# Two of four scans of a Mamba layer take their start value as a 513th column

## The chip, the cores and the metric

The kernel runs on one core of a Trainium2 chip. The metric is the device time of one execution in microseconds, in the runs before a median of 7167.19 us (three runs, 7165.84 to 7173.1). Engines: TensorE (PE; PEld is its weight load), VectorE (DVE), ScalarE (ACT), GpSimd (POOL) and SyncE (SP, which here issues DMAs). Each works off its own queue of instructions in order; semaphores make them wait for each other.

## The reference

Input: x, 4 images of 128 channels x 128 x 128. Layer 0 is a Mamba block over L = 16384 tokens per image, layer 1 a spectral layer (group norm, FFT, filter, inverse FFT). The change touches only the scan of layer 0:

```
A = -exp(A_log)                                  # 256 channels x 16 states
def step(h, (d_t, B_t, C_t, u_t)):               # over the 16384 tokens, in order
    dA = exp(d_t[:, :, None] * A)
    h  = h * dA + d_t[:, :, None] * B_t[:, None, :] * u_t[:, :, None]
    y  = einsum('bds,bs->bd', h, C_t)
```

Before it: an MLP, a projection, a convolution over four tokens with SiLU (u), and the projections to d (softplus), B and C. After it: y + u*D, times silu(z), an output projection, group norm, SiLU and a residual.

## The kernel before, in words

**Chunks, units, places, slots.** A chunk k is 512 tokens (T) of one image; 128 chunks run one after another (4 images x 32). The 256 channels x 16 states of a chunk are 4096 recurrences, which lie in 32 tiles of 128 partitions: 4 states (SQ) x 32 channels (DG). A unit (j, r) with j in 0, 1 and r in 0..3 holds four of these tiles, its places p = 0..3 (state group p, channel group place(r, p)). Two slots make a unit: the even slot n holds places 0 and 1, the odd slot places 2 and 3. So a chunk has 8 units and 16 slots (NP).

**One place.** ScalarE makes dA as exp(scale * delta) (exps, line 393): place 0 into SBUF (two buffers), places 1 to 3 into one PSUM bank each (one buffer). dB*u comes for places 1 to 3 from GpSimd as a product into the tile hb (dbu, line 363: 1536 columns per unit in one or two instructions), and for place 0 from TensorE as four transposes of the tile bt into the PSUM bank b0 (dbu_turn, line 383). VectorE then runs the recurrence with one tensor_tensor_scan over 512 columns (line 412). It starts from the last column of the same place in the chunk before (the tile st, one value per partition), or from the constant 0.0 in the first chunk of an image. Places 2 and 3 (by_vector) are scanned in place, in PSUM, multiplied by C on VectorE (line 414) into hb, and ScalarE copies their last column to st (line 415). Places 0 and 1 are scanned into the SBUF tile h, multiplied by C on GpSimd, both in one instruction of 1024 columns (line 419), and their last columns are copied on ScalarE a slot later (the copy of h; line 554 is the place that issues it). Place 1 of unit (1, 2) goes to VectorE in odd chunks that norm no image; place 2 of that unit goes to GpSimd in the chunks that do. TensorE sums the products over the states (sums, line 433) into y.

**What sets the order.** The order of work is written out by hand: a table todo[slot, phase] of small functions, issued slot by slot and phase by phase (lines 549 to 554), and kept as issued. Each engine works in that order. In a slot the phases are turn, sums, pe, exps, late, act, pool, dbu, early, gate, scans, dve, end:
- exps: in an even slot the exponentials of places 2 and 3 of the same unit, in an odd slot that of place 1 of the next unit.
- early (odd slots): the exponential of place 0 of the unit after the next.
- late: the copy of h's last columns.
- scans: both scans of the slot, place 0 before 1 and 2 before 3, then the products and, on ScalarE, the copies of VectorE's last columns.
- act and pool: the steps that prepare the next chunk (the table at lines 322 to 331): in slot 2 the SiLU of z and of u (lines 242, 239), in slot 6 the softplus (line 275), each with its table load; in slots 8 to 14 the bt activations (line 304), and so on. ScalarE's exponentials need a table of their own, so each of these two steps has a load ahead and one behind.
- dve: the gates (line 443, slots 2 and 10) and, in 16 chunks of each image but the first, the adds and statistics that norm the image before (lines 637, 641; slot 3).

E2 and E3 (exponentials of places 2 and 3) of a unit write the banks that the products of the unit before read; E1 writes the bank that S1 (scan of place 1) read.

A chunk that norms is one with norming(k); there are 48, and 80 plain ones. Layer 1 (block1) follows from about 6410 us on and has the time to the end.

Of the kernel before, what the change touches and what calls it, by code (L numbers as in the profile page):

```python
# [33 lines left out]
P = 128  # L34
# [5 lines left out]
EARLY = 2  # L40
KEEP = 4
LAG = 7
EPS = 1e-5


# [109 lines left out]
def block0(tc, s):  # L155
# [4 lines left out]
    with ExitStack() as ctx:  # L160
# [17 lines left out]
        def turn_bank(n):  # L178
            return pst.tile([P, T], F32, tag="pt", name=f"pt_{n}")

        st = {}
        stats, outs = s.stats, s.outs

# [163 lines left out]
        def by_vector(k, j, r, p):  # L347

            if norming(k):
                return p > 1 and (j, r, p) != (1, 2, 2)  # L350
            return p > 1 or (k % 2 == 1 and (j, r, p) == (1, 2, 1))

        def dbu(u):

            k, r = divmod(u, NH * NG)
            j, r = divmod(r, NG)
            d = st[k]
            hb = d["hb", j, r] = hpool.tile([P, ND, T], F32, tag="hb", name=f"hb_{k}_{j}_{r}")
            p = 1
            while p < NG:  # L360
                m = place(r, p)
                n = min(NG - p, ND - m)
                nc.gpsimd.tensor_tensor(  # L363
                    hb[:, p : p + n, :], d["du", j][:, m : m + n, :], d["B"][:, p - 1 : p - 1 + n, :], ALU.mult
                )
                p += n

        def pair(n):

# [5 lines left out]
        def dbu_turn(n):  # L375

            k, j, r, p = pair(n)
            d = st[k]
            if p == 0:
                b = d["b0"] = psd.tile([P, T], F32, tag="b0", name=f"b0_{k}_{j}_{r}")  # L380
                for t in range(NT):
                    src = d["bt"][:, t, j * ND + place(r, 0), :, :].rearrange("p s d -> p (s d)")
                    nc.tensor.transpose(b[:, t * P : (t + 1) * P], src, s.ident)  # L383

        def exps(n, qs):

            k, j, r, p = pair(n)
            d = st[k]
            for q in qs:
                m = place(r, p + q)  # L390
                c = (j * NG + p + q) * ND + m
                da = (psd if p + q else p2).tile([P, T], F32, tag=f"da{p + q}", name=f"da{p + q}_{k}_{j}_{r}")
                nc.scalar.activation(da, d["delta", j][:, m, :], AF.Exp, scale=s.amat[:, c : c + 1])  # L393
                d["da", j, r, p + q] = da

        def scans(n):


            k, j, r, p = pair(n)
            d = st[k]  # L400
            hb = d["hb", j, r]
            das = [d.pop(("da", j, r, p + q)) for q in range(2)]
            dve = [q for q in range(2) if by_vector(k, j, r, p + q)]
            pool = [q for q in range(2) if q not in dve]
            last = d["last", j, r, p] = tiny.tile([P, 2], F32, tag=f"st{j}_{r}_{p}", name=f"st_{k}_{j}_{r}_{p}")
            if pool:
                h = p2.tile([P, 2, T], F32, tag="h", name=f"h_{k}_{j}_{r}_{p}", bufs=3)
            for q in range(2):
                b = hb[:, p + q, :] if p + q else d.pop("b0")
                init = 0.0 if k % NCH == 0 else st[k - 1]["last", j, r, p][:, q : q + 1]  # L410
                o = das[q] if q in dve else h[:, q, :]
                nc.vector.tensor_tensor_scan(o, das[q], b, init, ALU.mult, ALU.add)  # L412
            for q in dve:
                nc.vector.tensor_tensor(hb[:, p + q, :], das[q], d["C"][:, p + q, :], ALU.mult)  # L414
                nc.scalar.copy(last[:, q : q + 1], das[q][:, T - 1 : T])  # L415
            if pool:
                q = slice(pool[0], pool[-1] + 1)
                ps = slice(p + pool[0], p + pool[-1] + 1)
                nc.gpsimd.tensor_tensor(hb[:, ps, :], h[:, q, :], d["C"][:, ps, :], ALU.mult)  # L419
                todo[n + 1, "late"].append(partial(nc.scalar.copy, last[:, q], h[:, q, T - 1]))  # L420

        def sums(u):

# [7 lines left out]
            for p in range(ND):  # L431
                m = place(r, p)
                nc.tensor.matmul(  # L433
                    y[m * DG : (m + 1) * DG, :], s.sel, d["hb", j, r][:, p, :], start=False, stop=r == NG - 1
                )

        def post(k):
# [101 lines left out]
        for n in range(n_chunks * NP):  # L539
            if n % 2 == 0:  # L540
                todo[n - 3, "early"].append(partial(exps, n, (0,)))
            todo[n - 1, "exps"].append(partial(exps, n, (1,) if n % 2 == 0 else (0, 1)))
            todo[n - 1, "turn"].append(partial(dbu_turn, n))
            todo[n, "scans"].append(partial(scans, n))
            if n % 2 == 0:
                todo[n - 2, "dbu"].append(partial(dbu, n // 2))
            else:
                todo[n + 2, "sums"].append(partial(sums, n // 2))
        slots = [n for n, _ in todo]
        with tc.manual_schedule():  # L550
            for n in range(min(slots), max(slots) + 1):
                for phase in ("turn", "sums", "pe", "exps", "late", "act", "pool", "dbu", "early", "gate", "scans", "dve", "end"):
                    for f in todo[n, phase]:
                        f()

# [500 lines left out]
```

## Time and profile before

| | us |
|---|---|
| median of the runs | 7167.19 |
| the profiled execution | 7175.45 |
| its span in the profile | 7173.6 |
| busy: DVE / POOL / ACT / PE | 6892.9 / 6892.5 / 6143.9 / 5904.2 |
| scans of VectorE, 4096, mean of one | 1.21 to 1.27 |
| products of VectorE (line 414), 2040, mean | 0.674 |
| products of GpSimd (line 419), 984 of 1024 columns and 88 of 512, mean | 2.363 and 1.276 |
| exponentials (line 393), 4096, mean | 0.700 |
| table loads, each | 1.283 |

Durations of one engine overlap by some 0.06 to 0.1 us, so its load is counted in steps from start to start. A line of the timeline gives the start, the length and the operation; x2 merges two of the same kind; the bracket tells how long the engine was idle before and what it waited for. In the chain of waits a share of an engine is time in which that engine had the work that ended last.

### The profile page before, as it was taken

The page shows a single profiled execution, that of the slowest core. Times are in us where ns is not written, and L with a number is a line of the kernel's source. Part 1 is how long each engine was busy: PE and PEld are TensorE (multiplying, and loading weights), DVE is VectorE, ACT ScalarE, POOL GpSimd, SP SyncE. Part 2 cuts the span into 40 slices and gives each one's busy share as a digit, 9 for nine tenths or more (in the row PEclk, how much of TensorE's full clock was granted, in tenths as well). Part 3 has the DMA queues.
Part 4 walks back from the last instruction along what each step waited for, and adds up shares of the span by engine and source line. Part 5 has one row for each costly group of instructions (what it writes and reads, how often), then busy time and mean ns, then how long its engine had stood idle before and what let it go on. Part 6 is the DMA issues. An engine that isn't in the chain of part 4 may idle for free.

```text
span 7173.6 us, 91384 instructions
## 1 busy us (share of the span) xinstructions
PE 5904.2 (82%) x26708; PEld 2626.8 (37%) x26708; DVE 6892.9 (96%) x7966; ACT 6143.9 (86%) x13658; POOL 6892.5 (96%) x3188
## 2 busy tenths in 40 slices
PE   6888888788787788888888788888887888867998
PEld 2333333233222233333333333333333333326888
DVE  6999999999999999999999999999999999989777
ACT  6888888888888888888888888898888888878876
POOL 6999999999999999999999999999999999988887
PEclk8888888888888889998989899999898899979999
DMA  5666666666777777777777777777777777769866
GB/s 139 160 160 152 163 159 151 165 159 165 191 176 192 179 171 176 172 184 175 189 196 186 188 176 175 178 177 184 189 191 194 177 179 177 172 164 306 236 185 162
DMA packets 905480, 1286.20 MB, mean 179 GB/s; under 512 B 81672, under 2 KB 356752, under 8 KB 904976
## 3 DMA queue, kind: packets, MB, share of 16 engines
q1 hardware_dynamic: 904832, 1280.09, 71.9%
q8 instruction: 210, 3.44, 0.2%
q14 instruction: 294, 2.41, 0.1%
q10 hardware_dynamic: 144, 0.26, 0.0%
HBM read 1023.45 MB, written 256.58 MB: 178 GB/s over the span
## 4 chain that ended last, share of the span: by engine, by line
DVE 41%; ACT 29%; issue 11%; PE 10%; DMA 5%; POOL 3%; SPq 1%; DVEq 0%; ACTq 0%; POOLq 0%
DVE da L412 20%; DVE h L412 12%; ACT da L393 12%; DVE hb L414 5%; ACT L393 3%; DMA rdelta<-dd 2%; ACT L275 2%; ACT delta L275 2%; ACT bt L304 2%; POOL hb L363 2%; DVE zs L443 1%; PE y L433 1%; POOL hb L419 1%; ACT L242 1%; DMA xt<-x 1%
## 5 line engine op out<-in xcount | busy, mean ns | idle before, releaser
L363 POOL TENSOR_TENSOR hb<-rdu,rB 128x1536 f32<-128x1536 f32 (+2 forms) x1536 | 3605.7, 2364 | 22.4 <-DMA rdelta<-dd 21.3
L393 ACT ACTIVATE da<-rdelta,amat 128x512 f32<-128x512 f32 x4096 | 2794.1, 700 | 138.3 <-DVE h L412 133.9
L419 POOL TENSOR_TENSOR hb<-h,rC 128x1024 f32<-128x1024 f32 (+1 forms) x1072 | 2435.0, 2274 | 88.8 <-DVE h L412 73.4
L412 DVE TENSOR_TENSOR_SCAN da<-da,st,hb 128x512 f32<-128x512 f32 x1976 | 2419.8, 1267 | 21.5 <-ACT da L393 14.3
L433 PE MATMUL y<-hb,sel 128*32 128x512 f32 x8192 | 1313.4, 717 | 2.9 <-POOL hb L419 2.7
L414 DVE TENSOR_TENSOR hb<-da,rC 128x512 f32<-128x512 f32 x2040 | 1296.1, 674 | 3.0
L412 DVE TENSOR_TENSOR_SCAN h<-da,st,b 128x512 f32<-128x512 f32 x992 | 1258.3, 1268 | 1.7 <-PE b L383 1.6
L412 DVE TENSOR_TENSOR_SCAN h<-da,st,hb 128x512 f32<-128x512 f32 x1000 | 1251.6, 1255 | 1.8 <-ACT da L393 1.8
L383 PE MATMUL b<-ident,bt 128*128 128x128 f32 x4096 | 748.4, 305 | 516.1 <-DVE h L412 390.6
L234 PE MATMUL pp_cv<-xm,wck 128*128 128x512 f32 x2048 | 1014.3, 640 | 1.6 <-ACT xm L217 0.8
L304 ACT ACTIVATE bt<-pt_dut,xdt 128x256 f32<-128x256 f32 x2048 | 839.4, 474 | 184.5 <-PE pt_dut L293 184.3
L383 PEld LDWEIGHTS b<-ident,bt 128*128 128x128 f32 x4096 | 531.3, 154 | 1017.1 <-DVE h L412 692.8
L415 ACT COPY st<-da 128x1 f32<-128x1 f32 x2040 | 273.1, 160 | 474.2 <-DVE hb L414 471.1
L234 PEld LDWEIGHTS pp_cv<-xm,wck 128*128 128x128 f32 x2048 | 395.9, 204 | 651.0 <-issue 422.1
L828 POOL TENSOR_TENSOR wb<-wb,term 128x1040 f32<-128x1040 f32 x192 | 461.0, 2401 | 70.8 <-ACT term L822 62.9
L293 PE MATMUL pt_dut<-ident,du 128*128 128x128 f32 x1024 | 232.4, 338 | 285.1 <-ACT xdt L286 174.9
L429 PE MATMUL y<-u,diag 128*128 128x512 f32 x512 | 303.0, 675 | 188.7 <-DVE zs L443 187.3
L293 PEld LDWEIGHTS pt_dut<-ident,du 128*128 128x128 f32 x1024 | 132.2, 162 | 604.8 <-POOL du L312 475.9
L393 ACT ACT_TABLE_LOAD x262 | 336.1, 1283 | 12.1 <-DMA rdelta<-dd 7.4
L312 POOL TENSOR_TENSOR du<-delta,u 128x512 f32<-128x512 f32 x256 | 318.8, 1267 | 25.8 <-ACT delta L275 25.8
L223 PE MATMUL pp_z<-xm,win 128*128 128x512 f32 x512 | 274.5, 634 | 51.8 <-ACT fq L497 46.2
L267 PE MATMUL pp_dt<-xd,wdt 8*128 8x512 f32 x512 | 284.8, 642 | 33.0 <-ACT pp_o L457 23.5
(160 smaller groups left out, 8139.8 us busy)
## 6 DMA issues: line engine op xcount, KB each, us to landing
rdelta<-dd SPq DMA_DIRECT2D x1024, 256.0 KB, 4.7
rdu<-dd SPq DMA_DIRECT2D x1024, 256.0 KB, 7.5
rC<-bc SPq DMA_DIRECT2D x512, 256.0 KB, 7.3
rB<-bc SPq DMA_DIRECT2D x512, 192.0 KB, 4.7
dd<-delta SPq DMA_DIRECT2D x256, 256.0 KB, 7.2
dd<-du SPq DMA_DIRECT2D x256, 256.0 KB, 5.7
ft<-in_filt_w SPq DMA_DIRECT2D x104, 520.0 KB, 7.0
ob<-o SPq DMA_DIRECT2D x128, 256.0 KB, 2.1
```

The costliest lines, as they stand in the source:

```text
L234: nc.tensor.matmul(ps["cv", j], w, d["xm"][:, t : t + T], start=t == 0, stop=t == KC - 1)
L293: nc.tensor.transpose(ps["dut"][:, 2 * t + j, :], d["du"][:, j, at : at + P], s.ident)
L304: nc.scalar.activation(d["bt"][:, 2 * h + t, :, q, :], src, AF.Copy, scale=d["xdt"][:, 2 * h + t, R + q : R + q + 1])
L312: nc.gpsimd.tensor_tensor(du, d["delta"][:, j, :], d["u"][:, j, :], ALU.mult)
L363: nc.gpsimd.tensor_tensor(hb[:, p : p + n, :], d["du", j][:, m : m + n, :], d["B"][:, p - 1 : p - 1 + n, :], ALU.mult)
L383: nc.tensor.transpose(b[:, t * P : (t + 1) * P], src, s.ident)
L393: nc.scalar.activation(da, d["delta", j][:, m, :], AF.Exp, scale=s.amat[:, c : c + 1])
L412: nc.vector.tensor_tensor_scan(o, das[q], b, init, ALU.mult, ALU.add)
L414: nc.vector.tensor_tensor(hb[:, p + q, :], das[q], d["C"][:, p + q, :], ALU.mult)
L419: nc.gpsimd.tensor_tensor(hb[:, ps, :], h[:, q, :], d["C"][:, ps, :], ALU.mult)
L433: nc.tensor.matmul(y[m * DG : (m + 1) * DG, :], s.sel, d["hb", j, r][:, p, :], start=False, stop=r == NG - 1)
L828: nc.gpsimd.tensor_tensor(wb, wb, u[n].terms[f], ALU.add)
```

## The change

- Places 1 and 2 of a unit are "carried": their scan runs over 513 columns from the constant 0.0. Column 0 of the second operand holds the start value, so the first step gives 0 * a + start. hb gets 513 columns per place, and a new step carry writes column 0 of places 1 and 2: on ScalarE a copy from the chunk before, in an image's first chunk a memset on GpSimd. The columns of dA must be 513 too: b0, dA of place 1 and dA of place 2 become three banks of one PSUM tile, band, and a carried scan reads from the last column of the bank before its own. The scan of place 2, in place, overwrites that column of place 1's bank. Where place 1 goes to VectorE, places 1 and 2 are not carried.
- The waits on band are set by hand (on_band): an instruction waits for the last one of each other engine on the same bank, and for none on other banks.
- The scans of an even slot run in the order 1, 0.
- Place 1 of unit (1, 2) goes to VectorE in all chunks that norm no image.
- The exponential of place 1 of the next unit is issued at the end of the odd slot's scans, behind late, early and carry; those three and scans now come before act, pool and dbu, and the products (with the copies of last columns) in a phase of their own after dbu.
- On TensorE the transposes for place 0 come after sums, but in units with r = 2 (of 0..3) before, as they were.

```diff
--- before.py
+++ after.py
@@ -40,6 +40,9 @@
 EARLY = 2
 KEEP = 4
 LAG = 7
+PHASES = (
+    "first turn", "sums", "turn", "pe", "exps", "late", "early", "carry", "scans", "act", "pool", "dbu", "products", "dve", "end"
+)
 EPS = 1e-5
 
 
@@ -178,6 +181,28 @@
         def turn_bank(n):
             return pst.tile([P, T], F32, tag="pt", name=f"pt_{n}")
 
+        band = psd.tile([P, 3 * T], F32, tag="band", name="band")
+        users = []
+
+        def on_band(engine, banks, made):
+
+            i = made.ins
+            seen = set()
+            for e, b, j in reversed(users):
+                if e == engine:
+                    continue
+                if not b & banks:
+                    tc.declare_no_dep(i, j, reason="another bank")
+                    continue
+                for bank in b & banks:
+                    if (e, bank) not in seen:
+                        seen.add((e, bank))
+                        tc.add_manual_dep(
+                            i, j.name, mybir.DependencyInfo(mybir.DependencyClass.Sync, mybir.DependencyReason.DATA),
+                            reason="same bank",
+                        )
+            users.append((engine, banks, i))
+            del users[:-40]
         st = {}
         stats, outs = s.stats, s.outs
 
@@ -348,22 +373,37 @@
 
             if norming(k):
                 return p > 1 and (j, r, p) != (1, 2, 2)
-            return p > 1 or (k % 2 == 1 and (j, r, p) == (1, 2, 1))
+            return p > 1 or (j, r, p) == (1, 2, 1)
 
         def dbu(u):
 
             k, r = divmod(u, NH * NG)
             j, r = divmod(r, NG)
             d = st[k]
-            hb = d["hb", j, r] = hpool.tile([P, ND, T], F32, tag="hb", name=f"hb_{k}_{j}_{r}")
+            hb = d["hb", j, r] = hpool.tile([P, ND, 1 + T], F32, tag="hb", name=f"hb_{k}_{j}_{r}")
             p = 1
             while p < NG:
                 m = place(r, p)
                 n = min(NG - p, ND - m)
                 nc.gpsimd.tensor_tensor(
-                    hb[:, p : p + n, :], d["du", j][:, m : m + n, :], d["B"][:, p - 1 : p - 1 + n, :], ALU.mult
+                    hb[:, p : p + n, 1:], d["du", j][:, m : m + n, :], d["B"][:, p - 1 : p - 1 + n, :], ALU.mult
                 )
                 p += n
+
+        def carried(k, j, r):
+
+            return () if by_vector(k, j, r, 1) else (1, 2)
+
+        def carry(u):
+
+            k, r = divmod(u, NH * NG)
+            j, r = divmod(r, NG)
+            if carried(k, j, r):
+                o = st[k]["hb", j, r][:, 1:3, 0]
+                if k % NCH == 0:
+                    nc.gpsimd.memset(o, 0.0)
+                else:
+                    nc.scalar.copy(o, st[k - 1]["last", j, r][:, 1:3])
 
         def pair(n):
 
@@ -377,10 +417,10 @@
             k, j, r, p = pair(n)
             d = st[k]
             if p == 0:
-                b = d["b0"] = psd.tile([P, T], F32, tag="b0", name=f"b0_{k}_{j}_{r}")
+                b = band[:, 0:T]
                 for t in range(NT):
                     src = d["bt"][:, t, j * ND + place(r, 0), :, :].rearrange("p s d -> p (s d)")
-                    nc.tensor.transpose(b[:, t * P : (t + 1) * P], src, s.ident)
+                    on_band("PE", {0}, nc.tensor.transpose(b[:, t * P : (t + 1) * P], src, s.ident))
 
         def exps(n, qs):
 
@@ -389,8 +429,13 @@
             for q in qs:
                 m = place(r, p + q)
                 c = (j * NG + p + q) * ND + m
-                da = (psd if p + q else p2).tile([P, T], F32, tag=f"da{p + q}", name=f"da{p + q}_{k}_{j}_{r}")
-                nc.scalar.activation(da, d["delta", j][:, m, :], AF.Exp, scale=s.amat[:, c : c + 1])
+                if p + q in (1, 2):
+                    da = band[:, (p + q) * T : (p + q + 1) * T]
+                else:
+                    da = (psd if p else p2).tile([P, T], F32, tag=f"da{p + q}", name=f"da{p + q}_{k}_{j}_{r}")
+                made = nc.scalar.activation(da, d["delta", j][:, m, :], AF.Exp, scale=s.amat[:, c : c + 1])
+                if p + q in (1, 2):
+                    on_band("ACT", {p + q}, made)
                 d["da", j, r, p + q] = da
 
         def scans(n):
@@ -402,22 +447,46 @@
             das = [d.pop(("da", j, r, p + q)) for q in range(2)]
             dve = [q for q in range(2) if by_vector(k, j, r, p + q)]
             pool = [q for q in range(2) if q not in dve]
-            last = d["last", j, r, p] = tiny.tile([P, 2], F32, tag=f"st{j}_{r}_{p}", name=f"st_{k}_{j}_{r}_{p}")
+            if p == 0:
+                d["last", j, r] = tiny.tile([P, ND], F32, tag=f"st{j}_{r}", name=f"st_{k}_{j}_{r}")
+            last = d["last", j, r][:, p : p + 2]
             if pool:
-                h = p2.tile([P, 2, T], F32, tag="h", name=f"h_{k}_{j}_{r}_{p}", bufs=3)
-            for q in range(2):
-                b = hb[:, p + q, :] if p + q else d.pop("b0")
-                init = 0.0 if k % NCH == 0 else st[k - 1]["last", j, r, p][:, q : q + 1]
-                o = das[q] if q in dve else h[:, q, :]
-                nc.vector.tensor_tensor_scan(o, das[q], b, init, ALU.mult, ALU.add)
+                h = p2.tile([P, 2, 1 + T], F32, tag="h", name=f"h_{k}_{j}_{r}_{p}", bufs=3)
+            order = (0, 1) if p else (1, 0)
+            for q in order:
+                if p + q in carried(k, j, r):
+                    a = band[:, (p + q) * T - 1 : (p + q + 1) * T]
+                    o = a if q in dve else h[:, q, :]
+                    made = nc.vector.tensor_tensor_scan(o, a, hb[:, p + q, :], 0.0, ALU.mult, ALU.add)
+                    on_band("DVE", {p + q - 1, p + q}, made)
+                    continue
+                b = hb[:, p + q, 1:] if p + q else band[:, 0:T]
+                init = 0.0 if k % NCH == 0 else st[k - 1]["last", j, r][:, p + q : p + q + 1]
+                o = das[q] if q in dve else h[:, q, 1:]
+                made = nc.vector.tensor_tensor_scan(o, das[q], b, init, ALU.mult, ALU.add)
+                if p + q < 3:
+                    on_band("DVE", {p + q}, made)
+            if p and n + 1 < n_chunks * NP:
+                exps(n + 1, (1,))
+            d["scanned"] = k, j, r, p, hb, das, dve, pool, last, h if pool else None
+
+        def products(n):
+
+            d = st[n // NP]
+            k, j, r, p, hb, das, dve, pool, last, h = d.pop("scanned")
             for q in dve:
-                nc.vector.tensor_tensor(hb[:, p + q, :], das[q], d["C"][:, p + q, :], ALU.mult)
-                nc.scalar.copy(last[:, q : q + 1], das[q][:, T - 1 : T])
+                made = [
+                    ("DVE", nc.vector.tensor_tensor(hb[:, p + q, 1:], das[q], d["C"][:, p + q, :], ALU.mult)),
+                    ("ACT", nc.scalar.copy(last[:, q : q + 1], das[q][:, T - 1 : T])),
+                ]
+                if p + q < 3:
+                    for engine, i in made:
+                        on_band(engine, {p + q}, i)
             if pool:
                 q = slice(pool[0], pool[-1] + 1)
                 ps = slice(p + pool[0], p + pool[-1] + 1)
-                nc.gpsimd.tensor_tensor(hb[:, ps, :], h[:, q, :], d["C"][:, ps, :], ALU.mult)
-                todo[n + 1, "late"].append(partial(nc.scalar.copy, last[:, q], h[:, q, T - 1]))
+                nc.gpsimd.tensor_tensor(hb[:, ps, 1:], h[:, q, 1:], d["C"][:, ps, :], ALU.mult)
+                todo[n + 1, "late"].append(partial(nc.scalar.copy, last[:, q], h[:, q, T]))
 
         def sums(u):
 
@@ -431,7 +500,7 @@
             for p in range(ND):
                 m = place(r, p)
                 nc.tensor.matmul(
-                    y[m * DG : (m + 1) * DG, :], s.sel, d["hb", j, r][:, p, :], start=False, stop=r == NG - 1
+                    y[m * DG : (m + 1) * DG, :], s.sel, d["hb", j, r][:, p, 1:], start=False, stop=r == NG - 1
                 )
 
         def post(k):
@@ -539,17 +608,20 @@
         for n in range(n_chunks * NP):
             if n % 2 == 0:
                 todo[n - 3, "early"].append(partial(exps, n, (0,)))
-            todo[n - 1, "exps"].append(partial(exps, n, (1,) if n % 2 == 0 else (0, 1)))
-            todo[n - 1, "turn"].append(partial(dbu_turn, n))
+            if n % 2 or n == 0:
+                todo[n - 1, "exps"].append(partial(exps, n, (0, 1) if n % 2 else (1,)))
+            todo[n - 1, "first turn" if n // 2 % NG == 2 else "turn"].append(partial(dbu_turn, n))
             todo[n, "scans"].append(partial(scans, n))
+            todo[n, "products"].append(partial(products, n))
             if n % 2 == 0:
                 todo[n - 2, "dbu"].append(partial(dbu, n // 2))
+                todo[n - 1, "carry"].append(partial(carry, n // 2))
             else:
                 todo[n + 2, "sums"].append(partial(sums, n // 2))
         slots = [n for n, _ in todo]
         with tc.manual_schedule():
             for n in range(min(slots), max(slots) + 1):
-                for phase in ("turn", "sums", "pe", "exps", "late", "act", "pool", "dbu", "early", "gate", "scans", "dve", "end"):
+                for phase in PHASES:
                     for f in todo[n, phase]:
                         f()
 
```

## The prediction

> **Names.** A chunk is 512 tokens and has eight units (r = 0 to 7 here), each of two slots. A unit has four places: scans S0, S1 and exponentials E0, E1 belong to its even slot, S2, S3, E2, E3 and the vector products M2, M3 to its odd slot. A prime marks the next unit.
>
> **What bounds the kernel now.** I read the page's busy shares, then its chain of waits, then the timeline of VectorE and ScalarE over one plain chunk.
>
> ```profile
> PE 5904.2 (82%) x26708; PEld 2626.8 (37%) x26708; DVE 6892.9 (96%) x7966; ACT 6143.9 (86%) x13658; POOL 6892.5 (96%) x3188
> ...
> DVE 41%; ACT 29%; issue 11%; PE 10%; DMA 5%; POOL 3%; SPq 1%; DVEq 0%; ACTq 0%; POOLq 0%
> ```
>
> VectorE and GpSimd look equally full. But the stretches of the windows view show VectorE busy 1499.40 of 1500 us (from 150 to 1650), GpSimd 1486.39: VectorE never stops. The chain nevertheless gives ScalarE 29%, so there are places where both are late together. The timeline shows one (first ScalarE, then VectorE; columns: start, duration, what):
>
> ```profile
> 1487.48 0.16 ACT L415 COPY st<-da 128x1 f32<-128x1 f32 x1 [0.44 <-DVE hb L414]
> 1487.53 1.31 ACT L393 ACTIVATE da<-rdelta,amat 128x512 f32<-128x512 f32 x2
> 1488.86 1.28 ACT L242 ACT_TABLE_LOAD   x1
> 1490.15 1.06 ACT L242 ACTIVATE zs<-zs 128x1024 f32<-128x1024 f32 x1
> 1491.12 1.25 ACT L239 ACTIVATE u<-pp_cv,conv_b 128x512 f32<-128x512 f32 x2
> 1492.38 1.28 ACT L393 ACT_TABLE_LOAD   x1
> 1493.67 0.69 ACT L393 ACTIVATE da<-rdelta,amat 128x512 f32<-128x512 f32 x1
> 1494.30 0.18 ACT L554 COPY st<-h 128x2 f32<-128x2 f32 x1
> 1494.38 0.72 ACT L393 ACTIVATE da<-rdelta,amat 128x512 f32<-128x512 f32 x1
> ```
> ```profile
> 1492.67 1.27 DVE L414 TENSOR_TENSOR hb<-da,rC 128x512 f32<-128x512 f32 x2
> 1493.85 1.27 DVE L412 TENSOR_TENSOR_SCAN h<-da,st,b 128x512 f32<-128x512 f32 x1
> 1495.04 1.26 DVE L412 TENSOR_TENSOR_SCAN h<-da,st,hb 128x512 f32<-128x512 f32 x1
> ```
>
> The copy at 1487.48 waited for M3: ScalarE can't run ahead of that point, since E2 and E3 reuse the PSUM banks that M2 and M3 read. From there ScalarE works without a gap: E2, E3, the two SiLU activations of slot 2 between two table loads, and only then E1' for unit r=2 (1493.67 to 1494.36). S0' starts at 1493.85, S1' at 1495.04: E1' is 0.68 us early, and that only because S1' comes second. After it stand the copy of S0/S1's last columns (1494.30) and E0 of the unit after that (1494.38).
>
> The softplus of slot 6 makes a second such place, before unit r=4:
>
> ```profile
> 1503.83 1.28 ACT L393 ACT_TABLE_LOAD   x1
> 1505.12 0.69 ACT L393 ACTIVATE da<-rdelta,amat 128x512 f32<-128x512 f32 x1
> ```
> ```profile
> 1505.65 1.27 DVE L412 TENSOR_TENSOR_SCAN h<-da,st,b 128x512 f32<-128x512 f32 x1
> ```
>
> E1' ends at 1505.81; S0' started at 1505.65, S1' starts at 1506.84: 1.03 us early.
>
> **The change part by part.**
>
> *Cheaper scans.* The first chunk of the second image (1640 to 1674 us are in it) starts from zero, so its scans have a constant as start. The view of line 412 from 1640 to 1710 us (min/median/max ns) sets both kinds side by side:
>
> ```profile
> L412 DVE TENSOR_TENSOR_SCAN da<-da,hb x12: 1204/1206/1231, 1642.3 to 1672.3; 128x512 f32<-128x512 f32 x12
> L412 DVE TENSOR_TENSOR_SCAN da<-da,st,hb x12: 1262/1264/1286, 1677.0 to 1709.0; 128x512 f32<-128x512 f32 x12
> ...
> L412 DVE TENSOR_TENSOR_SCAN h<-da,hb x6: 1192/1194/1198, 1641.1 to 1670.1; 128x512 f32<-128x512 f32 x6
> ...
> L412 DVE TENSOR_TENSOR_SCAN h<-da,st,hb x6: 1253/1254/1259, 1675.8 to 1706.0; 128x512 f32<-128x512 f32 x6
> ```
>
> The constant saves 58 ns in place (S2) and 60 ns into h (S1). Column 513 costs at most 1206/512 = 2.4 ns; 57 ns remain. No row shows an operand that runs over two PSUM banks; it may cost nothing, or all of the gain (the pointer scan, 1264, is the nearest dearer row). I take nothing and keep the other end. Count: 80 plain chunks x 7 units + 48 chunks that also norm an image x 8 = 944 units, two scans each, 1888; 56 of them (4 first chunks x 14) have a constant already. 1832 x 0.057 = **-104 us**, all on VectorE's path.
>
> *One more product on VectorE.* In the 40 even plain chunks place 1 of unit (1, 2) goes from GpSimd to VectorE. Two products take 1.27 and one 0.68, so one more is 0.59: 40 x 0.59 = **+24**. GpSimd sheds 40 x (2363 - 1276 ns) = 43 us, off the path. In the 40 odd chunks that product now follows S0 instead of the S1 that it needs; the 0.12 us by which it misses the usual overlap (2022.28 against 2020.98 + 1.18 in the timeline) go: **-5**.
>
> *S1 first.* S1' now starts where S0' did, 1.19 us earlier, so all that it needs is due 1.19 earlier. Products of GpSimd need both scans, no change. S0 ends 1.18 later, and TensorE's four transposes for b0 (0.6 us) wait for it; b0 is due again one unit (5.9 us) later, some 3.5 us after S0, so this is covered even with the sums (1.9 us) now issued ahead of the transposes in three of four units; the odd slots' pe steps stand behind the same two, whichever is first.
>
> *E1' moved.* In the odd slot ScalarE ran E1', copy of h, act steps, bt copies, E0. Now it runs copy of h, E0, the new carry copy, E1', then act steps. One wait is added: E1' needs S2 (which reads and overwrites the last column of its bank), where it needed S1. S2 ends 1.18 (S3) + 1.18 (M2, M3) = 2.36 us ahead of S1', E1' takes 0.69: covered in units where ScalarE idles. Queued behind it are the act steps (at most four bt copies, 1.57 us), then the copies of M2 and M3 and E2', due 2.36 after M3; 0.1 + 0.69 + 1.57 = 2.36 lies just at M3's end, covered. Moving E0 and the copy ahead is not covered at the two places above. E1' starts later by their start-to-start steps, 0.08 (1494.30 to 1494.38) and 0.62 (two exponentials take 1.31, one 0.69), and by the carry copy: its shape and memory are those of the copy of h, so 0.08 (0.18 if it didn't overlap).
>
> First place: ScalarE is free for the copy at 1493.67; + 0.08 + 0.62 + 0.08 + 0.69 = 1495.14; about 0.10 from ScalarE's end to VectorE's start (estimate: where the trace has VectorE waiting for an exponential the gap is 0.09 to 0.10) gives 1495.24. S1' is due at 1493.85 less 0.11 (two cheaper scans since M3) = 1493.74. Stall **1.50 us**. In chunks that also norm an image, VectorE has two adds and two statistics more in slot 3: E1' ends at 2053.88, S1' starts at 2055.57, 1.69 early instead of 0.68; stall 1.50 - 1.01 = 0.49. Second place: 1505.12 + 1.47 + 0.10 = 1506.69 against 1505.54: **1.15 us**, in both kinds of chunk. The other six units: the same sum leaves E1' 0.1 us early in the tightest (r = 5 and 6 of plain chunks) and over 1 us early in the rest.
>
> Sum: 79 x 1.50 + 48 x 0.49 + 127 x 1.15 = 118 + 24 + 146 = **+288 us** (the last chunk prepares none). A stall isn't won back: ScalarE is held at the next M3 again.
>
> *Waits, carry, layout.* 944 carry copies or memsets; at 0.08 they fit ScalarE's gaps outside the two places. The carry copy may also wait for GpSimd's dB products in the same tile; those end about 2.8 us before the unit starts (1496.98 against 1499.75), in time. Rows of 513 start off the old boundaries; GpSimd's line 899 works in rows of 65, with 1298 ns for 520 elements against 1276 for 512: no cost.
>
> The ScalarE row for table switches is 1.28 us, with the next activation 0.01 us later (1492.38 + 1.28, then 1493.67). The Trainium skill, page "ScalarE: Activation LUTs", section "What ACT_TABLE_LOAD costs", states a drain of about 1.38 us behind each load, 2.66 in all, which would weigh on all that is put behind a switch. By the page the two switches would make each place 2.76 us later, 254 x 2.76 = 701 us more; this trace shows no such drain, and I go by the trace.
>
> **Total.** -104 + 24 - 5 + 288 = +203. The profiled execution took 7175.45 us (span 7173.6), so 7378; the median, 7167.19, lies 8.3 lower (0.1%), and I put the sum on it: **7370 us**, 2.8% slower. The second layer is untouched.
>
> **The rivals.**
> - *E1' in time at both places* (13%): then the scans' gain stands alone: -104 + 24 - 5 = -85, 7082 us, faster. It decides where E1' ends before S0's old start, so ScalarE's stretch from M3 would have to be 1.5 and 1.2 us shorter. For it: in six of eight units E1' is in time. Against: ScalarE's stretch has no gap in the rows, and its start is held by M3.
> - *Only one place stalls, or both by half* (5%): about +145 in place of 288: 7167 + 60 = 7227.
> - *The scan over two banks gains nothing* (10%): +104, while S1' is due 0.11 later, -28: 7370 + 76 = 7446. For it: no row shows such an operand.
> - *The change doesn't do what it says* (2%): the one tile over three banks is still waited for as a whole, so b0's transposes wait for M2: 0.1 + 0.66 + 0.1 against M3's 0.59, about 0.3 us x 1024 units more: 7680.
> - *My forecast* (70%): 7370, own range 7340 to 7410 (the carry copy at 0.18 adds 25; the tight units at 0.1 us late add 16; ScalarE's steps some 0.1 us shorter take 25).
>
> **How the numbers follow.** 0.2%, 14 us, is about what a measurement of this kernel can tell from no change. Faster 0.14, within 0.2% 0.03, slower 0.83: the first rival, what lies between it and the second, and the rest. The range takes in the half stall and the two-bank end with the dear carry copy: 7225 to 7490; it leaves out the first rival and the whole-tile waits, 15%.
>
> **What would show it.** Right: scans from a constant with medians near 1197 (into h) and 1208 (in place); VectorE idle of about 290 us before S1, ended by ScalarE's exponential, 1.5 and 1.15 us at a time, twice a chunk and only there; plain chunks of some 50.8 us from first S0 to first S0, where the timeline now has 48.4 (even) and 49.1 (odd). Wrong: no idle before S1 (first rival), scans of 1260 (third), VectorE waiting in every unit (fourth), or idle ended by the carry copy or GpSimd instead.

## The result and the profile after

The changed kernel takes 7519.27 us (median of four runs, 7515.2 to 7520.28) against 7166.51 us before: ratio 1.0487, 95% interval 1.0471 to 1.0504, 353 us slower. The profiled execution took 7520.28 us, its span is 7518.4. The forecast was 7370, its range ended at 7490.

The page's busy shares:

```profile
PE 6080.4 (81%) x26708; PEld 2661.6 (35%) x26708; DVE 6916.0 (92%) x8006; ACT 6300.4 (84%) x14614; POOL 6701.9 (89%) x3216
```

VectorE's busy time hardly moved (6892.9 to 6916.0), its share fell from 96% to 92%: nearly all of the added time is idle time of the engine that bounds the kernel. The chain of waits breaks off early in this profile (its shares add up to 13%), so I read the groups of VectorE by shape (count, busy us, mean ns, then idle time ahead of them and what ended it):

```profile
L466 DVE TENSOR_TENSOR_SCAN h<-da,st,band 128x512 f32<-128x512 f32 x992 | 1247.3, 1257 | 9.0 <-DVE band L466 1.4
L460 DVE TENSOR_TENSOR_SCAN h<-band,hb 128x513 f32<-128x513 f32 x992 | 1207.6, 1217 | 296.2 <-issue 114.2 <-POOL hb L388 104.7 <-POOL hb L404 43.8
L460 DVE TENSOR_TENSOR_SCAN band<-band,hb 128x513 f32<-128x513 f32 x896 | 1102.4, 1230 | 78.9 <-ACT band L436 7.0 <-DVE h L466 2.7 <-ACT st L626 0.5
```

These are S0, S1 and S2 (48 scans of place 2 that go to GpSimd are among S1's 992). S1 has 296.2 us of idle time ahead of it, near the 290 forecast, but 43.8 of them are one wait at the start of the kernel, which the kernel before has ahead of S0 (38.4); the two places have less than forecast. S2 has 78.9, which was not forecast. The releasers named for S1 (issue, GpSimd's hb) are inferred and differ between places that are alike; the timeline settles it, at unit r=2 and r=4 of a plain chunk, VectorE first:

```profile
1540.93 0.68 DVE L479 TENSOR_TENSOR hb<-da,rC 128x512 f32<-128x512 f32 x1
1542.86 1.22 DVE L460 TENSOR_TENSOR_SCAN h<-band,hb 128x513 f32<-128x513 f32 x1 [1.25 <-POOL hb L388]
1544.00 1.26 DVE L466 TENSOR_TENSOR_SCAN h<-da,st,band 128x512 f32<-128x512 f32 x1
1545.39 1.23 DVE L460 TENSOR_TENSOR_SCAN band<-band,hb 128x513 f32<-128x513 f32 x1
...
1554.29 0.68 DVE L479 TENSOR_TENSOR hb<-da,rC 128x512 f32<-128x512 f32 x1
1555.81 1.23 DVE L460 TENSOR_TENSOR_SCAN h<-band,hb 128x513 f32<-128x513 f32 x1 [0.84 <-issue]
```
```profile
1540.08 1.28 ACT L436 ACT_TABLE_LOAD   x1
1541.37 0.72 ACT L436 ACTIVATE da<-rdelta,amat 128x512 f32<-128x512 f32 x1
1542.00 0.18 ACT L406 COPY hb<-st 128x2 f32<-128x2 f32 x1
1542.08 0.68 ACT L436 ACTIVATE band<-rdelta,amat 128x512 f32<-128x512 f32 x1
```

ScalarE ends the exponential of place 1 at 1542.76, and S1 starts 0.10 us later. At r=4 it ends at 1555.73, S1 starts at 1555.81. The same holds over the whole trace: S1 starts 0.05 to 0.15 us after the end of an exponential in all 120 units r=2 and in 126 of the 127 units r=4 in which it waits. GpSimd's product for the unit of 1542.86 had ended at 1537.25. So E1' is what S1 waits for, twice a chunk, with medians of 1.41 us at r=2 in plain chunks, 0.42 in norming ones, and 0.84 at r=4. The second thing to see is S0 at 1544.00: it ends at 1545.26, and S2 starts at 1545.39, 1.39 after S0's start. Before, S2 followed the scan ahead of it (S1, at 1495.04 in the prediction's lines) by 1.17 and overlapped it:

```profile
1496.21 2.45 DVE L412 TENSOR_TENSOR_SCAN da<-da,st,hb 128x512 f32<-128x512 f32 x2
```

Over the trace the step from S0's start to S2's is 1.361 us at the median where S2 follows S0 directly (675 units); before, the step into S2 was 1.174.

Summed over the trace by unit, VectorE's idle time ahead of S1 is 113 us at r=2, 107 at r=4 and 27 at r=1. At r=1 S1 starts within 0.2 us of the end of TensorE's transposes in 46 of the 47 units in which it waits. A plain chunk takes 52.13 us (48.37 and 49.12 before), a norming one 51.93 (50.30).

### The profile page after: what moved, and what is told of

The parts are those of the page before. It is cut to its first block, busy times and chain, and to the rows that moved or that the text cites. A ratio compares the mean times of both kernels' runs of the same rounds, so it can differ in the third digit from the quotient of the medians.

```text
span 7518.4 us, 94560 instructions
## 1 busy us (share of the span) xinstructions
PE 6080.4 (81%) x26708; PEld 2661.6 (35%) x26708; DVE 6916.0 (92%) x8006; ACT 6300.4 (84%) x14614; POOL 6701.9 (89%) x3216
## 5 line engine op out<-in xcount | busy, mean ns | idle before, releaser
L436 ACT ACTIVATE band<-rdelta,amat 128x512 f32<-128x512 f32 x2048 | 1425.2, 696 | 182.2 <-DVE band L460 179.0
L460 DVE TENSOR_TENSOR_SCAN h<-band,hb 128x513 f32<-128x513 f32 x992 | 1207.6, 1217 | 296.2 <-issue 114.2
L436 ACT ACTIVATE da<-rdelta,amat 128x512 f32<-128x512 f32 x2048 | 1444.9, 706 | 4.2 <-issue 1.1
L423 PE MATMUL band<-ident,bt 128*128 128x128 f32 x4096 | 775.5, 319 | 602.9 <-DVE h L466 585.1
L466 DVE TENSOR_TENSOR_SCAN h<-da,st,band 128x512 f32<-128x512 f32 x992 | 1247.3, 1257 | 9.0 <-DVE band L466 1.4
L466 DVE TENSOR_TENSOR_SCAN da<-da,st,hb 128x512 f32<-128x512 f32 x992 | 1255.5, 1266 | 0.0
L259 PE MATMUL pp_cv<-xm,wck 128*128 128x512 f32 x2048 | 1037.3, 654 | 202.3 <-ACT zs L253 201.2
L460 DVE TENSOR_TENSOR_SCAN band<-band,hb 128x513 f32<-128x513 f32 x896 | 1102.4, 1230 | 78.9 <-ACT band L436 7.0
L423 PEld LDWEIGHTS band<-ident,bt 128*128 128x128 f32 x4096 | 502.3, 157 | 1618.7 <-DVE h L466 1238.7
L329 ACT ACTIVATE bt<-pt_dut,xdt 128x256 f32<-128x256 f32 x2048 | 834.8, 471 | 200.3 <-PE pt_dut L318 200.3
L479 DVE TENSOR_TENSOR hb<-band,rC 128x512 f32<-128x512 f32 x1056 | 710.0, 672 | 0.0
L479 DVE TENSOR_TENSOR hb<-da,rC 128x512 f32<-128x512 f32 x1024 | 693.7, 677 | 1.6
```

Of the source, the lines that this page charges most:

```text
L259: nc.tensor.matmul(ps["cv", j], w, d["xm"][:, t : t + T], start=t == 0, stop=t == KC - 1)
L329: nc.scalar.activation(d["bt"][:, 2 * h + t, :, q, :], src, AF.Copy, scale=d["xdt"][:, 2 * h + t, R + q : R + q + 1])
L423: on_band("PE", {0}, nc.tensor.transpose(b[:, t * P : (t + 1) * P], src, s.ident))
L436: made = nc.scalar.activation(da, d["delta", j][:, m, :], AF.Exp, scale=s.amat[:, c : c + 1])
L460: made = nc.vector.tensor_tensor_scan(o, a, hb[:, p + q, :], 0.0, ALU.mult, ALU.add)
L466: made = nc.vector.tensor_tensor_scan(o, das[q], b, init, ALU.mult, ALU.add)
```

## The experiments

Times are medians of four runs or more, and the ratio is against runs of the kernel before on the same chip. Those took 7172 to 7174 us beside the experiments and 7166.51 beside the changed kernel, so a difference to the changed kernel is good to some 8 us. Some edits are shown in part ("..."). "-" and "+" lines are against the changed kernel, unless it says against the kernel before.

**1. The old order in the even slot**

```diff
-            order = (0, 1) if p else (1, 0)
+            order = (0, 1)
```

> The changed kernel with the scans of an even slot in the old order, 0 before 1. Theory (the 353 us are late exponentials of place 1, some 240, an own-engine wait of S2 in each unit without a gate, some 140, and a scan gain of only some 70): S1 is due 1.13 us later, so the idle time before unit r=4 goes (0.92) and that before r=2 shrinks by 1.13 in plain chunks and by 0.5 in norming ones: 89 + 24 + 117 = 230 us less, 7290; S2 still waits for the end of the scan ahead of it, now S1. Rival (S1 is held by GpSimd's dB products, as the waits view names them): also less, but the idle time moves to the same GpSimd release instead of vanishing; at least 7350.

Measured: 7321.84, ratio 1.0211 (1.0196 to 1.0226): 197 us less, not 230. S1's and S0's rows of VectorE's groups:

```profile
L466 DVE TENSOR_TENSOR_SCAN h<-da,st,band 128x512 f32<-128x512 f32 x992 | 1262.0, 1272 | 43.0 <-PE band L423 42.5
...
L460 DVE TENSOR_TENSOR_SCAN h<-band,hb 128x513 f32<-128x513 f32 x992 | 1187.8, 1201 | 15.3 <-ACT band L436 12.6 <-POOL hb L404 2.4
L460 DVE TENSOR_TENSOR_SCAN band<-band,hb 128x513 f32<-128x513 f32 x896 | 1102.3, 1230 | 81.3 <-ACT band L436 10.5 <-DVE h L460 1.4 <-ACT da L436 0.5
```

S1's idle time is all but gone (296.2 to 15.3; the 43.8 at the start now stand ahead of S0, 38.7) and hasn't moved to GpSimd. S2's 81.3 stays. S0's 43.0 is the wait for TensorE's transposes, before unit r=1, of which the changed kernel has 27 us ahead of S1; these 16 more, and some 12 that are left at r=2, are most of what the 230 fell short by. TensorE is late there because its convolution waits for a PSUM bank that the copies of z free: 201.2 us of TensorE's idle time ahead of pp_cv end with zs in the changed kernel, 200.3 here and 0.6 in the kernel before. Those copies now stand behind E1', which waits for S2; in runs 8 and 9, where they stand ahead of E1', the wait is back at 0.6.

**2. Place 1 alone carried**

```diff
-            return () if by_vector(k, j, r, 1) else (1, 2)
+            return () if by_vector(k, j, r, 1) else (1,)
...
-                o = st[k]["hb", j, r][:, 1:3, 0]
+                o = st[k]["hb", j, r][:, 1:2, 0]
...
-                    nc.scalar.copy(o, st[k - 1]["last", j, r][:, 1:3])
+                    nc.scalar.copy(o, st[k - 1]["last", j, r][:, 1:2])
```

> The changed kernel with place 1 alone carried; place 2 starts from its pointer over 512 columns and no longer writes the bank that S1 read. Theory: the step from S0 to S2 falls from 1.36 to 1.18 us, some 0.2 x 688 = 138 less; S2 loses its gain, 30 more; the exponential at r=4 is 0.2 later against its scan, 27 more: 7438. Rival (the step from S0 to S2 is longer because S1 runs ahead of S0, whatever S2 writes): 7519 + 30 = 7549.

Measured: 7550.77, ratio 1.0531 (1.0513 to 1.0548). My theory fails here, in that S2's overwritten column isn't the cause: S2 now writes its own bank alone and still waits; the step from S0 stays at 1.361. The time is the rival's (7549), but its reason, that S1 runs ahead of S0, falls with run 5.

```profile
L466 DVE TENSOR_TENSOR_SCAN band<-band,st,hb 128x512 f32<-128x512 f32 x1020 | 1314.5, 1289 | 87.0 <-ACT band L436 6.7 <-DVE h L466 3.2 <-ACT st L480 0.5
```

**3. The exponential of place 1 ahead of the copy of h, E0 and carry**

```diff
-    "first turn", "sums", "turn", "pe", "exps", "late", "early", "carry", "scans", "act", "pool", "dbu", "products", "dve", "end"
+    "first turn", "sums", "turn", "pe", "exps", "scans", "late", "early", "carry", "act", "pool", "dbu", "products", "dve", "end"
```

> The changed kernel with scans ahead of late, early and carry, so that ScalarE makes the next unit's exponential of place 1 before the copy of h, the exponential of place 0 and the carry copy. Theory: it is 0.78 us earlier at both places: idle before r=2 from 1.48 to 0.7 (plain) and 0.42 to 0 (norming), before r=4 from 0.92 to 0.14: 79 x 0.78 + 48 x 0.42 + 127 x 0.78 = 181 less, 7338. Rival (GpSimd's dB products hold S1): no change, 7519.

Measured: 7605.22, ratio 1.0607 (1.0591 to 1.0622): worse than the changed kernel. The expectation had forgotten that S1 needs column 0 too, and the carry copy now stood last:

```profile
L460 DVE TENSOR_TENSOR_SCAN h<-band,hb 128x513 f32<-128x513 f32 x992 | 1208.6, 1218 | 374.7 <-ACT hb L406 131.0 <-POOL hb L388 64.8 <-PE band L423 55.4
```

The same steps stand between the second table load and S1, only the last one has changed. By unit the idle time fell at r=2 (113 to 76 us) and rose at r=4 (107 to 157) and at r=1 (27 to 86), where TensorE's transposes are late. The copy of h, E0 and the carry copy now stand behind E1', which waits for S2; that this is what made r=4 worse isn't shown by itself. The next run has both in front.

**4. Carry and the exponential of place 1 in front**

```diff
-    "first turn", "sums", "turn", "pe", "exps", "late", "early", "carry", "scans", "act", "pool", "dbu", "products", "dve", "end"
+    "first turn", "sums", "turn", "pe", "exps", "carry", "scans", "late", "early", "act", "pool", "dbu", "products", "dve", "end"
```

> The changed kernel with carry and scans ahead of late and early: ScalarE now makes both things that S1 needs, the carry copy and the exponential of place 1, before the copy of h and the exponential of place 0 (the run with the exponential alone in front left the carry copy behind them, and S1 waited for that). Theory: S1 is released 0.70 us earlier at both places: 79 x 0.70 + 48 x 0.42 + 127 x 0.70 = 164 less, 7355; less is won where steps of ScalarE behind the exponential come later for it. Rival (S1 is held by GpSimd's dB products or by TensorE): no change, 7519.

Measured: 7415.98, ratio 1.0336 (1.032 to 1.0351): 103 us less. Ahead of S1 at r=2 the idle time falls from 113 us to 17, at r=4 from 107 to 55; at r=1, where TensorE's transposes are late, it grows from 27 to 74. That is 148 less and 47 more.

```profile
L460 DVE TENSOR_TENSOR_SCAN h<-band,hb 128x513 f32<-128x513 f32 x992 | 1208.6, 1218 | 192.2 <-PE band L423 64.4 <-POOL hb L404 42.7 <-ACT band L436 32.4
```

So ScalarE's order does set the stall, and GpSimd, whose work and order are unchanged, doesn't. The price is paid at r=1: TensorE's wait for the copies of z is 259.5 us here.

**5. The swap alone, on the kernel before**

```diff
-            for q in range(2):
+            for q in (0, 1) if p else (1, 0):
                 b = hb[:, p + q, :] if p + q else d.pop("b0")
```

> The kernel before with one edit: the even slot's scans run 1 before 0. Theory: exponential 1 ends 0.6 us after S0's old start before r=2 of plain chunks and 0.25 after it before r=4: 79 x 0.6 + 127 x 0.25 = 80 us more, 7247, and no longer step from S0 to S2, since place 2 writes nothing that place 1 read. Rival (the swap itself lengthens that step by 0.2 in each unit): 80 + 140 = 220 more, 7387.

Measured: 7247.02, ratio 1.0106 (1.0091 to 1.0121), the expected 7247. S0 and S2 (the first of the two scans of the second line) have no gap between them, and the step is 1.172 us at the median:

```profile
1499.62 1.25 DVE L412 TENSOR_TENSOR_SCAN h<-da,st,b 128x512 f32<-128x512 f32 x1
1500.79 2.44 DVE L412 TENSOR_TENSOR_SCAN da<-da,st,hb 128x512 f32<-128x512 f32 x2
```

The swap takes the slack of E1' away, as the prediction reckoned, and does nothing to S2. The longer step thus belongs to neither the swap (this run) nor the overwritten column (run 2). What is left is the band: in it S0, S1 and S2 use one PSUM tile.

**6. Place 3 ahead of place 2 in the odd slot**

```diff
-            order = (0, 1) if p else (1, 0)
+            order = (1, 0)
...
-            for q in dve:
+            for q in dve[::-1] if p else dve:
...
-                todo[n - 1, "exps"].append(partial(exps, n, (0, 1) if n % 2 else (1,)))
+                todo[n - 1, "exps"].append(partial(exps, n, (1, 0) if n % 2 else (1,)))
```

> The changed kernel with the odd slot worked 3 before 2: scans, products, last columns and exponentials. Theory (S2 waits for the end of the band's last reader, S0, because one engine's uses of the one tile band are ordered as a whole): S3, which is not on the band, now stands between, so the wait is covered: 0.2 x 688 = 138 less, the place before r=4 0.2 later against its scan, 27 more: 7408; the exponential of place 1 waits for S2, which now ends 1.18 later, and can cost some 20 to 60 more where ScalarE has many steps behind it. Rival (the longer step is what two-bank operands or a changed order of places cost VectorE): the step stays with S2 or goes to S3, 7519 or more.

Measured: 7569.08, ratio 1.0552 (1.0536 to 1.0568). The total went against me and the wait went as the theory says:

```profile
L466 DVE TENSOR_TENSOR_SCAN da<-da,st,hb 128x512 f32<-128x512 f32 x992 | 1264.4, 1275 | 10.1 <-ACT da L436 5.9 <-issue 3.2 <-POOL hb L488 0.9
...
L460 DVE TENSOR_TENSOR_SCAN h<-band,hb 128x513 f32<-128x513 f32 x992 | 1210.0, 1220 | 503.6 <-ACT band L436 274.7 <-PE band L423 81.8 <-issue 47.4
L460 DVE TENSOR_TENSOR_SCAN band<-band,hb 128x513 f32<-128x513 f32 x896 | 1083.5, 1209 | 0.0
```

S2's idle time is 0.0, with the same operands over two banks; S3, now behind S0, has 10.1. But S1's grew to 503.6. E1' waits for S2, which ends a step later, and in order behind E1' stand the output's activations (slot 5) and, after them, the copies that start the softplus stretch. At r=4 S1 then waits 1.8 us, not 0.84, and the wait at r=1 grows to 136 us in all.

**7. b0 in a tile of its own, place 2 alone carried**

```diff
-        band = psd.tile([P, 3 * T], F32, tag="band", name="band")
+        band = psd.tile([P, 2 * T], F32, tag="band", name="band")
...
-                b = band[:, 0:T]
+                b = d["b0"] = psd.tile([P, T], F32, tag="b0", name=f"b0_{k}_{j}_{r}")
...
-            return () if by_vector(k, j, r, 1) else (1, 2)
+            return () if by_vector(k, j, r, 1) else (2,)
```

(Places 1 and 2 are banks 0 and 1 of the band; carry copies one column.)

> The changed kernel with b0 in a PSUM tile of its own, the band of two banks (places 1 and 2), and place 2 alone carried; place 1 starts from its pointer over 512 columns. S0 no longer touches the band. Theory (one engine's uses of one tile are ordered as a whole, so S2 waited for S0 because S0 read the same tile): S2 waits for S1, which S0 covers, and the idle time of 0.10 to 0.13 us before it goes: 138 less; S1 loses its gain, 38 more; the place before r=4 is 0.2 later against its scan, 27 more: 7446. Rival (S2 waits because it overwrites the column that S1 read, whatever S0 uses): the wait stays, 7519 + 38 = 7557.

Measured: 7424.15, ratio 1.0349 (1.0332 to 1.0367), on the theory's side (7446) and far from the rival (7557).

```profile
L460 DVE TENSOR_TENSOR_SCAN band<-band,hb 128x513 f32<-128x513 f32 x896 | 1087.4, 1214 | 6.8 <-ACT band L436 6.6
```

```profile
1549.00 1.26 DVE L466 TENSOR_TENSOR_SCAN h<-da,st,b 128x512 f32<-128x512 f32 x1
1550.17 1.21 DVE L460 TENSOR_TENSOR_SCAN band<-band,hb 128x513 f32<-128x513 f32 x1
```

S2 here overwrites the column that S1 read, in the order S1, S0, S2, and starts 1.17 after S0, without a wait. S0 no longer uses the tile.

Unit (1, 2) of plain chunks shows the same with nothing carried at all. There S1, from a pointer and in place, writes place 1's bank, and S0, from a pointer too, reads b0. In the changed kernel both banks lie in the tile band, here b0 has its own tile:

```profile
1568.20 1.28 DVE L466 TENSOR_TENSOR_SCAN band<-band,st,hb 128x512 f32<-128x512 f32 x1
1569.58 1.28 DVE L466 TENSOR_TENSOR_SCAN h<-da,st,band 128x512 f32<-128x512 f32 x1
```
```profile
1592.42 1.28 DVE L466 TENSOR_TENSOR_SCAN band<-band,st,hb 128x512 f32<-128x512 f32 x1
1593.61 1.26 DVE L466 TENSOR_TENSOR_SCAN h<-da,st,b 128x512 f32<-128x512 f32 x1
```

The step is 1.38 in the changed kernel (first fence) and 1.19 in this run (second). So the gap was VectorE waiting for its own last use of the tile band, whichever bank that was in, where one of the two uses writes. Two reads don't wait: S1 and S0 of a carried unit both read the band, and their step is 1.133. The waits set by hand (on_band) pass over uses by the same engine and leave those to the framework.

**8. The waits taken away**

```diff
-            order = (0, 1) if p else (1, 0)
+            order = (1, 0) if p else (0, 1)
...
-    "first turn", "sums", "turn", "pe", "exps", "late", "early", "carry", "scans", "act", "pool", "dbu", "products", "dve", "end"
+    "first turn", "turn", "sums", "pe", "exps", "late", "carry", "act", "pool", "scans", "early", "dbu", "products", "dve", "end"
```

(With the odd slot's products and exponentials 3 before 2, as in run 6.)

> The changed kernel with the even slot in the old order 0, 1, the odd slot 3 before 2, TensorE's transposes always ahead of sums, and on ScalarE in the odd slot: copy of h, carry, act and pool steps, exponential of place 1, exponential of place 0. Theory: all three added waits are gone and what is left is the scans' gain as the changed kernel's steps show it (1.174 to 1.133 for S1, 1.175 to 1.142 for S2, 68 us) and one more product in 40 chunks (19): 7167 - 49 = 7118. Rival (the 513-column scans can't beat the pointer scans, since their waits come back elsewhere): 7167 or more.

Measured: 7141.13, ratio 0.9955 (0.9939 to 0.9972), faster than before.

```profile
L466 DVE TENSOR_TENSOR_SCAN h<-da,st,band 128x512 f32<-128x512 f32 x992 | 1267.9, 1278 | 2.1 <-PE band L423 2.0
L460 DVE TENSOR_TENSOR_SCAN h<-band,hb 128x513 f32<-128x513 f32 x992 | 1196.6, 1206 | 22.7 <-ACT band L436 18.8 <-POOL hb L404 3.4 <-issue 0.2
L460 DVE TENSOR_TENSOR_SCAN band<-band,hb 128x513 f32<-128x513 f32 x896 | 1086.2, 1212 | 0.0
```

The idle time is all but gone at all three places: 2.1, 22.7 and 0.0. The act steps now stand ahead of E1', where ScalarE would wait for S2 anyway. Most of the 23 us above the expectation is the unit (1, 2) in plain chunks: places 1 and 2 start from pointers there, and S1, which writes the band, waits for S0, which reads it. Their step is 1.41 against 1.19 before; times 80 this is 18 us.

**9. That unit's product back on GpSimd**

```diff
-            return p > 1 or (j, r, p) == (1, 2, 1)
+            return p > 1
```

(In chunks that norm no image; against run 8.)

> As the run with all three waits taken away, and the product of place 1 of unit (1, 2) on GpSimd in all chunks that norm no image (in the kernel before: in every second one). GpSimd's product of two places takes 2.18 us in the changed kernel where it took 2.36, so it has room: VectorE sheds 80 x 0.59 and gains 80 more pairs of cheap scans: 53 less, 7065. Rival (GpSimd becomes the bound): no gain, 7118 or more.

Measured: 7061.64, ratio 0.9842 (0.9828 to 0.9857): 1.6% faster than the kernel before, the best version found. A plain chunk takes 47.63 us.

**10. The layout alone, on the kernel before**

```diff
-            hb = d["hb", j, r] = hpool.tile([P, ND, T], F32, tag="hb", name=f"hb_{k}_{j}_{r}")
+            hb = d["hb", j, r] = hpool.tile([P, ND, 1 + T], F32, tag="hb", name=f"hb_{k}_{j}_{r}")
...
-                h = p2.tile([P, 2, T], F32, tag="h", name=f"h_{k}_{j}_{r}_{p}", bufs=3)
+                h = p2.tile([P, 2, 1 + T], F32, tag="h", name=f"h_{k}_{j}_{r}_{p}", bufs=3)
...
```

(Products and scans use columns 1 to 512, and the last columns of a unit share one tile, as in the changed kernel.)

> The kernel before with the layout of the changed one and nothing else: hb and h have 513 columns per place, of which the first isn't used, and the last columns of a unit share one tile of four. Theory: GpSimd's product of two places takes 2.18 us instead of 2.36 because its two rows of 512 no longer lie end to end, and the time stays within 0.2% of 7167, since VectorE is the bound. Rival (the product is faster in the changed kernel because VectorE idles beside it): 2.36 here.

Measured: 7178.72, ratio 1.0008 (0.9999 to 1.0017): no change in time.

```profile
L421 POOL TENSOR_TENSOR hb<-h,rC 128x1024 f32<-128x1024 f32 x984 | 2154.8, 2190 | 252.9 <-DVE h L414 248.9 <-DVE total L696 1.7 <-DMA spec<-fq 0.9
```

GpSimd's product takes 2190 ns with the layout alone (2363 before), and the time it saves (170 us) becomes waiting for VectorE (idle 252.9 ahead of it, 88.8 before): VectorE was the bound before.

## Why the prediction was wrong

The direction and its main cause were right, the size was not: +353 us against +203. Half of the 353 are waits of VectorE for itself, which the sum put at nothing.

- **Cheaper scans, -104: right.** The two ends were "all of the gain lost to two banks" and "57 ns kept". Steps from start to start, as medians over the trace: S1 to S0 is 1.191 us from a pointer (run 5) and 1.133 over 513 columns from the constant (the changed kernel); S2 to S3 is 1.175 before and, where S2 doesn't wait, 1.117 (run 7): 58 ns each, over two banks. The durations are not those of the sign that was set (1197 and 1208 ns; medians 1215 and 1232), because a scan's duration also depends on what stands ahead of it. S1 from a pointer takes 1256 behind a scan (before) and 1275 behind a product (run 5), and it stands behind a product now. S2 stands behind its wait; without that it takes 1210 (run 7).
- **One more product, +24 - 5:** not run alone. Run 9 took the product and that unit's uncarried scans away in 80 chunks for 79 us, more than the 53 expected; the unit's wait in run 8 (18 us) went with them.
- **E1' late at two places, +288: right in kind, somewhat too large.** 113 us at r=2 (118 + 24 forecast) and 107 at r=4 (146 forecast), and each stall also loses the usual overlap of some 0.08, 21 us in all: 241. The place at r=4 came out 0.2 us shorter because S2's wait in the unit ahead makes S1 due later: without that wait (run 7) the median idle time there is 1.01 in place of 0.84. Run 5 bears the term out: with the swap alone the same sum gave 80 and the chip 75 to 80. The times given for a norming chunk, 2053.88 and 2055.57, are not in the trace; the nearest norming chunk has 2043.05 and 2044.74, and the 1.69 between them is right.
- **"S1 first" and "Waits, carry, layout": the step that failed.** These parts asked what each engine waits for from the others, and put VectorE's wait for itself at nothing without a reason. Putting b0, E1 and E2 into one tile made S2 wait for the end of S0. The price per unit: the step from S0 to S2 is 1.361 where run 5 has 1.172 (0.10 to 0.13 idle, the rest lost overlap), and S2's own step is 0.026 longer (1.142 against 1.117), some 0.215; 688 units (944 less the 256 where a gate stands between) make 148 us. Unit (1, 2) of plain chunks has two more such waits of 0.19 each, S0 for S1 and S2 for the product of place 1: some 31 us. The fourth rival had the cause, the one tile still waited for as a whole, but looked for it at TensorE's transposes, at 0.3 us and in all 1024 units, and got 2%. The signs lay in the diff: on_band skips users of its own engine ahead of its test for another bank.
- **Act steps behind E1', "covered": nearly.** The copies of z behind E1' delayed TensorE's convolution, and the transposes behind it came late before r=1: 27 us in the changed kernel, 43 to 136 in runs 1, 3, 4 and 6. The sign "twice a chunk and only there" failed here too.
- **The sum:** -104 + 19 + 241 + 148 + 31 + 27 = 362, against 345 between the two profiled spans (353 between the medians). Some 15 us of idle time that the kernel before has ahead of S2 at r=6 and 7 (22 us) are no longer there, which makes it 347. The terms from 148 on are worked out from the traces; runs 1, 6, 7, 8 and 9 show them come and go.
- **Layout, no cost: right**, and GpSimd gained (run 10).

The rival that GpSimd's dB products hold S1, which the waits view suggests, falls with the end of E1' just ahead of S1 in the timeline and with run 4, which changes ScalarE's order alone. That VectorE's uses of one tile are ordered as a whole is shown by runs 2, 5, 6 and 7 together. Why the framework does this wasn't looked into, and the direct test, telling it that VectorE's uses of different banks of the band don't concern each other, wasn't run. The swap of the even slot isn't needed for the gain: run 8 has the old order and the cheap scans.

## What to carry to other kernels

When several buffers are joined into one tile so that an operand can run across them, list the waits of each engine for itself as well as those for others, and put an instruction that doesn't use the tile between two that do. Before a step is moved in an in-order queue, write down for the instruction that needs it the whole stretch from the last point where that queue was held, at the busiest slot and not at the mean one: here two places a chunk with 0.7 and 1.0 us of slack cost some 240 us. A gain of 58 ns per instruction on the bounding engine is real, but it is smaller than one lost overlap (some 80 ns).

## What the runs showed of the hardware

- A wait of VectorE for its own scan, with nothing else missing, costs some 0.2 us: the step from S0 to S2 is 1.361 us with it (changed kernel) and 1.172 without (runs 5 and 7), of which 0.10 to 0.13 is idle time and the rest the overlap of some 0.08 that back-to-back scans have.
- A scan from a constant is 58 ns shorter than one from a per-partition value (steps of 1.133 against 1.191 and 1.117 against 1.175). A 513th column, whose operand runs over two PSUM banks, takes nothing that can be seen from this: scans of 512 columns from the constant have steps of 1.130 and 1.115 in the first chunks of run 5.
- GpSimd's product of two rows of 512 took 2363 ns where the rows lie end to end in h and in the output, and 2190 where they are 513 apart there (run 10; C lies end to end in both). Its dB products, whose inputs still lie end to end and whose output rows are 513 apart, stayed at 2363 for 1024 columns. The cause wasn't sought.
